# Upper-triangle self-products of 4096 rows: batch rows adjacent on a partition, 64 KB store packets, three large buffers, and single-row instructions shared by VectorE and ScalarE

## The chip, the cores and the metric

One core of one Trainium2 chip. The metric is the device time of one execution in microseconds; executions of a kernel agree here within 0.07%. All runs quoted are at full granted clock. Profiles are of one execution; its span, from first to last instruction, is about 1.8 us below the device time.

## The reference, cut to what matters

```python
def reference(inputs):                       # float32 [4096, 256]
    dot = jnp.einsum('bi,bj->bij', inputs, inputs)
    iu, ju = jnp.triu_indices(256)
    return dot[:, iu, ju]                    # float32 [4096, 32896]
```

Row i of the triangle of one batch row is `x[i] * x[i:256]`, a run of 256 - i products. The input has 4.19 MB, the output 538.97 MB: this is a kernel that writes.

## The kernel before

The batch rows are cut into 8 groups of 4 tiles of 128 rows. A partition holds four rows that are 128 rows apart in HBM, and a chunk is 2048 columns (the last 2176) of them. So one store of 4 MB consists of 512 separate runs of 8 KB. Four buffers rotate.

```python
x_in = x.rearrange("(g t p) d -> g p t d", t=GROUP, p=P)
x_out = out.rearrange("(g t p) c -> g p t c", t=GROUP, p=P)
# ... all eight x tiles are loaded at the start ...
for g in range(groups):
    xt = xs[g]
    for c, (lo, hi) in enumerate(zip(borders, borders[1:])):
        o = opool.tile([P, GROUP, widest], F32, tag="o", name=f"o_{g}_{c}")
        for i, j, col, length in runs(d, lo, hi):
            a = col - lo
            if length <= SHORT:              # 64: one VectorE instruction for four rows
                nc.vector.tensor_tensor(...)
                continue
            for t in range(GROUP):           # else one per row, every fourth on ScalarE
                # ... dst, src, factor ...
                if t == GROUP - 1:
                    nc.scalar.activation(dst, src, AF.Copy, scale=factor)
                else:
                    nc.vector.tensor_scalar(dst, src, factor, None, ALU.mult)
        nc.sync.dma_start(x_out[g][:, :, lo:hi], o[:, :, : hi - lo])
```

Of the kernel before, what the change touches and what calls it, by code (L numbers as in the profile page):

```python
# [1 line left out]

# [4 lines left out]

F32 = mybir.dt.float32
AF = mybir.ActivationFunctionType
ALU = mybir.AluOpType  # L10

P = 128
UNIT = 128      # columns: chunk borders are multiples of it, 512 bytes in HBM
CHUNKS = 16     # pieces that an output row is cut into
GROUP = 4       # batch tiles of 128 rows that are computed and stored together
SHORT = 64      # runs up to this length take one instruction for the whole group


def chunk_borders(width: int) -> list[int]:
    units = width // UNIT  # L20
    borders = [units * c // CHUNKS * UNIT for c in range(CHUNKS)]
    return borders + [width]


def runs(d: int, lo: int, hi: int):
    """The runs of output columns [lo, hi) with one first factor: (i, j, column, length), for
    x[i] * x[j : j + length]. Row i of the upper triangle has j from i on."""
    at = 0
    for i in range(d):
        a, b = max(at, lo), min(at + d - i, hi)  # L30
        if a < b:
            yield i, i + a - at, a, b - a
        at += d - i


@with_exitstack
def kernel(
    ctx: ExitStack, tc: tile.TileContext, x: bass.AP, out: bass.AP
):
    """out[n, :] = the upper triangle, row by row, of the outer product of x[n] with itself.  # L40

    Batch rows lie on the partitions. The input stays on chip; the output is made chunk by chunk
    and each chunk goes out in one store while the next ones are computed."""
    nc = tc.nc
    n, d = x.shape
    width = out.shape[1]
    assert n % (P * GROUP) == 0 and width == d * (d + 1) // 2 and width % UNIT == 0
    groups = n // (P * GROUP)
    borders = chunk_borders(width)
    widest = max(b - a for a, b in zip(borders, borders[1:]))  # L50

    xpool = ctx.enter_context(tc.tile_pool(name="x", bufs=1))
    opool = ctx.enter_context(tc.tile_pool(name="o", bufs=4))

    x_in = x.rearrange("(g t p) d -> g p t d", t=GROUP, p=P)
    x_out = out.rearrange("(g t p) c -> g p t c", t=GROUP, p=P)

    xs = []
    for g in range(groups):
        xt = xpool.tile([P, GROUP, d], F32, tag=f"x{g}", name=f"x{g}")  # L60
        nc.sync.dma_start(xt, x_in[g])
        xs.append(xt)

    for g in range(groups):
        xt = xs[g]
        for c, (lo, hi) in enumerate(zip(borders, borders[1:])):
            o = opool.tile([P, GROUP, widest], F32, tag="o", name=f"o_{g}_{c}")
            for i, j, col, length in runs(d, lo, hi):
                a = col - lo
                if length <= SHORT:  # L70
                    nc.vector.tensor_tensor(  # L71
                        o[:, :, a : a + length],
                        xt[:, :, j : j + length],
                        xt[:, :, i : i + 1].to_broadcast([P, GROUP, length]),
                        ALU.mult,
                    )
                    continue
                for t in range(GROUP):
                    dst = o[:, t, a : a + length]
                    src = xt[:, t, j : j + length]  # L80
                    factor = xt[:, t, i : i + 1]
                    # Of four such instructions one goes to the Scalar engine.
                    if t == GROUP - 1:
                        nc.scalar.activation(dst, src, AF.Copy, scale=factor)  # L84
                    else:
                        nc.vector.tensor_scalar(dst, src, factor, None, ALU.mult)  # L86
            nc.sync.dma_start(x_out[g][:, :, lo:hi], o[:, :, : hi - lo])  # L87


# [1 line left out]
_INS = ["r_inputs"]  # L91
_OUTS = [((4096, 32896), "float32")]


# [20 lines left out]
```

## Time and profile before

| | before |
|---|---|
| device time, median of 4 | 1312.78 us (1312.46 to 1312.98) |
| VectorE / ScalarE instructions | 5272 / 1553 |
| data packets on the store queue | 71808, most of 8 KB |
| output stores | 128, 4 buffers |

The lines that carry the argument stand in the prediction. Two more parts of the page, first the chain of work that ended last (shares of the span by engine), then the three large groups of instructions (line, engine, operation, shapes, count, busy us, mean ns, idle us before them):

```profile
DMA 54%; DVE 43%; issue 0%; DVEq 0%; SPq 0%
...
L86 DVE TENSOR_SCALAR o<-x 128x256 f32<-128x256 f32 (+44 forms) x4656 | 989.7, 291 | 111.4 <-DMA out_dram<-o 106.9
L84 ACT ACTIVATE o<-x 128x105 f32<-128x105 f32 (+59 forms) x1552 | 503.5, 411 | 764.4 <-DMA out_dram<-o 762.0
L71 DVE TENSOR_TENSOR o<-x 128x112 f32<-128x112 f32 (+51 forms) x616 | 137.1, 284 | 60.0 <-DMA out_dram<-o 60.0
```

The chain's 43% of VectorE looks like a second bound; the prediction says why it is not one.

### The profile page before, as it was taken

How to read it: one execution, taken by the hardware profiler on the slowest of the kernel's cores; microseconds unless marked ns; L12 is line 12 of the kernel's file. 1: busy time of each engine (PE TensorE's matmuls, PEld its weight loads, DVE VectorE, ACT ScalarE, POOL GpSimd, SP SyncE). 2: the span in 40 equal slices, each digit the busy share in tenths (PEclk: the TensorE clock that was granted, in tenths of full speed). 3: DMA queues.
4: the chain of work that ended last, by engine and by line, in shares of the span. 5: the costliest groups of instructions: out<-in, count | busy, mean ns of one | idle time of the engine just before them, and what ended most of it. 6: DMA issues, size and time to landing. Idle time of an engine off the chain costs nothing.

```text
span 1310.8 us, 7383 instructions
## 1 busy us (share of the span) xinstructions
DVE 1116.7 (85%) x5272; ACT 504.8 (39%) x1553; POOL 0.2 (0%) x4
## 2 busy tenths in 40 slices
DVE  8889977899778997789977899778996789967893
ACT  5345234442344423345333443334433443334430
POOL 0000000000000000000000000000000000000000
DMA  9999999999999999999999999999999999999996
GB/s 370 428 428 421 420 419 419 419 420 419 419 419 419 420 419 420 419 419 419 419 420 419 419 419 419 419 418 419 420 419 419 419 419 418 420 419 419 419 419 274
DMA packets 71865, 543.64 MB, mean 415 GB/s; under 512 B 2176, under 2 KB 6272, under 8 KB 6272
## 3 DMA queue, kind: packets, MB, share of 16 engines
q1 hardware_dynamic: 71808, 543.17, 100.0%
q14 instruction: 57, 0.47, 0.1%
HBM read 4.19 MB, written 538.97 MB: 414 GB/s over the span
## 4 chain that ended last, share of the span: by engine, by line
DMA 54%; DVE 43%; issue 0%; DVEq 0%; SPq 0%
DMA out_dram<-o 54%; DVE o L86 34%; DVE o L71 9%; DMA x<-in_r_inputs_dram 0%; DVEq L71 0%; DVEq L86 0%; SPq L87 0%; DVEq L111 0%
## 5 line engine op out<-in xcount | busy, mean ns | idle before, releaser
L86 DVE TENSOR_SCALAR o<-x 128x256 f32<-128x256 f32 (+44 forms) x4656 | 989.7, 291 | 111.4 <-DMA out_dram<-o 106.9
L84 ACT ACTIVATE o<-x 128x105 f32<-128x105 f32 (+59 forms) x1552 | 503.5, 411 | 764.4 <-DMA out_dram<-o 762.0
L71 DVE TENSOR_TENSOR o<-x 128x112 f32<-128x112 f32 (+51 forms) x616 | 137.1, 284 | 60.0 <-DMA out_dram<-o 60.0
L84 ACT ACT_TABLE_LOAD x1 | 1.3, 1283 | 0.7 <-PEq L102 0.7
L102 POOL MEMSET const-bfloat16-1.0<- 128x1 bf16 x1 | 0.1, 102 | 0.0
L102 POOL MEMSET const-uint8-127<- 128x1 uint8 x1 | 0.1, 101 | 0.0
L102 POOL MEMSET const-float32-0.0<- 128x1 f32 x1 | 0.1, 98 | 0.2 <-issue 0.2
L102 POOL MEMSET const-float32-1.0<- 128x1 f32 x1 | 0.1, 98 | 0.0
## 6 DMA issues: line engine op xcount, KB each, us to landing
out_dram<-o SPq DMA_DIRECT2D x120, 4096.0 KB, 31.5
out_dram<-o SPq DMA_DIRECT2D x8, 4352.0 KB, 22.6
x<-in_r_inputs_dram SPq DMA_DIRECT2D x8, 512.0 KB, 8.6
```

The costliest lines, as they stand in the source:

```text
L71: nc.vector.tensor_tensor(o[:, :, a : a + length], xt[:, :, j : j + length], xt[:, :, i : i + 1].to_broadcast([P, GROUP, length]), ALU.mult,)
L84: nc.scalar.activation(dst, src, AF.Copy, scale=factor)
L86: nc.vector.tensor_scalar(dst, src, factor, None, ALU.mult)
L102: nc = _bacc.Bacc("TRN2", target_bir_lowering=False, num_devices=1)
```

## The change

The intent is long contiguous packets. A partition takes 32 adjacent batch rows, whose output is one contiguous stretch of 4 MiB + 16 KiB. It is cut into 64 chunks of 64.8 or 65.0 KB per partition after a first tile that goes out in four growing pieces. Three buffers of 64 KB per partition hold 192 KB. Rows in a chunk no longer line up, so every product row is one instruction; a running cost estimate gives it to VectorE or ScalarE. The diff, cut to its core:

```diff
-    xpool = ctx.enter_context(tc.tile_pool(name="x", bufs=1))
-    opool = ctx.enter_context(tc.tile_pool(name="o", bufs=4))
-    x_in = x.rearrange("(g t p) d -> g p t d", t=GROUP, p=P)
-    x_out = out.rearrange("(g t p) c -> g p t c", t=GROUP, p=P)
+    xpool = ctx.enter_context(tc.tile_pool(name="x", bufs=3))
+    opool = ctx.enter_context(tc.tile_pool(name="o", bufs=3))
+    x_in = x.rearrange("(p r) d -> p r d", p=P)
+    x_out = out.rearrange("(p r) c -> p (r c)", p=P)
 ...
+SLOT = 16384
+FIRST = [1024, 3072, 7168, 15360]
+ROWS = 4
 ...
+    def multiply(self, dst, src, factor, length: int):
+        v = self.vector + 130 + 0.51 * length
+        s = self.scalar + 187 + 0.83 * length
+        if v <= s:
+            self.vector = v
+            self.nc.vector.tensor_scalar(dst, src, factor, None, ALU.mult)
+        else:
+            self.scalar = s
+            self.nc.scalar.activation(dst, src, AF.Copy, scale=factor)
 ...
+    borders = [0] + even_borders(FIRST[-1], total, -(-rest // SLOT))
+    for c, (lo, hi) in enumerate(zip(borders, borders[1:])):
+        if lo // width // ROWS > len(xs) - 3:
+            load()                           # the next four input rows of each partition
+        o = opool.tile([P, SLOT], F32, tag="o", name=f"o_{c}")
+        cuts = [0] + FIRST if c == 0 else [lo, hi]
+        for a, b in zip(cuts, cuts[1:]):
+            shares.even()
+            for row, i, j, at, length in runs(d, a, b):
+                # ... shares.multiply(...) ...
+            nc.sync.dma_start(x_out[:, a:b], o[:, a - lo : b - lo])
```

More of the change, by code (lines that the diff above doesn't have):

```diff
@@ L12, with even_borders, __init__, even @@
 P = 128
-UNIT = 128
-CHUNKS = 16
-GROUP = 4
-SHORT = 64
-def chunk_borders(width: int) -> list[int]:
-    units = width // UNIT
-    borders = [units * c // CHUNKS * UNIT for c in range(CHUNKS)]
-    return borders + [width]
-def runs(d: int, lo: int, hi: int):
-    at = 0
-    for i in range(d):
-        a, b = max(at, lo), min(at + d - i, hi)
-        if a < b:
-            yield i, i + a - at, a, b - a
-        at += d - i
+UNIT = 64
+def even_borders(lo: int, hi: int, pieces: int) -> list[int]:
+    units = (hi - lo) // UNIT
+    return [lo + units * c // pieces * UNIT for c in range(pieces)] + [hi]
+def runs(d: int, lo: int, hi: int):
+    width = d * (d + 1) // 2
+    for row in range(lo // width, (hi + width - 1) // width):
+        at = row * width
+        for i in range(d):
+            a, b = max(at, lo), min(at + d - i, hi)
+            if a < b:
+                yield row, i, i + a - at, a, b - a
+            at += d - i
+class Shares:
+    def __init__(self, nc):
+        self.nc = nc
+        self.vector = self.scalar = 0.0
+    def even(self):
+        self.vector = self.scalar = 0.0
+    def multiply(self, dst, src, factor, length: int):
[10 more added lines that the diff above has]
+ROWS = 4
 @with_exitstack
@@ L46 @@
     width = out.shape[1]
-    assert n % (P * GROUP) == 0 and width == d * (d + 1) // 2 and width % UNIT == 0
-    groups = n // (P * GROUP)
-    borders = chunk_borders(width)
-    widest = max(b - a for a, b in zip(borders, borders[1:]))
-    xpool = ctx.enter_context(tc.tile_pool(name="x", bufs=1))
-    opool = ctx.enter_context(tc.tile_pool(name="o", bufs=4))
-    x_in = x.rearrange("(g t p) d -> g p t d", t=GROUP, p=P)
-    x_out = out.rearrange("(g t p) c -> g p t c", t=GROUP, p=P)
-    xs = []
@@ L59 @@
-    for g in range(groups):
-        xt = xpool.tile([P, GROUP, d], F32, tag=f"x{g}", name=f"x{g}")
-        nc.sync.dma_start(xt, x_in[g])
-        xs.append(xt)
-    for g in range(groups):
-        xt = xs[g]
-        for c, (lo, hi) in enumerate(zip(borders, borders[1:])):
-            o = opool.tile([P, GROUP, widest], F32, tag="o", name=f"o_{g}_{c}")
-            for i, j, col, length in runs(d, lo, hi):
-                a = col - lo
-                if length <= SHORT:
-                    nc.vector.tensor_tensor(
-                        o[:, :, a : a + length],
-                        xt[:, :, j : j + length],
-                        xt[:, :, i : i + 1].to_broadcast([P, GROUP, length]),
-                        ALU.mult,
-                    )
-                    continue
-                for t in range(GROUP):
-                    dst = o[:, t, a : a + length]
-                    src = xt[:, t, j : j + length]
-                    factor = xt[:, t, i : i + 1]
-                    if t == GROUP - 1:
-                        nc.scalar.activation(dst, src, AF.Copy, scale=factor)
-                    else:
-                        nc.vector.tensor_scalar(dst, src, factor, None, ALU.mult)
-            nc.sync.dma_start(x_out[g][:, :, lo:hi], o[:, :, : hi - lo])
@@ new lines, with load @@
+    assert n % P == 0 and width == d * (d + 1) // 2
+    per = n // P
+    total = per * width
+    assert per % ROWS == 0 and total % UNIT == 0
+    xpool = ctx.enter_context(tc.tile_pool(name="x", bufs=3))
+    opool = ctx.enter_context(tc.tile_pool(name="o", bufs=3))
+    x_in = x.rearrange("(p r) d -> p r d", p=P)
+    x_out = out.rearrange("(p r) c -> p (r c)", p=P)
+    xs = []
+    def load(first_apart: bool = False):
+        g = len(xs)
+        if g * ROWS >= per:
+            return
+        xt = xpool.tile([P, ROWS, d], F32, tag="x", name=f"x_{g}")
+        cuts = [0, 1, ROWS] if first_apart else [0, ROWS]
+        for a, b in zip(cuts, cuts[1:]):
+            nc.sync.dma_start(xt[:, a:b, :], x_in[:, g * ROWS + a : g * ROWS + b, :])
+        xs.append(xt)
@@ new lines @@
+    load(first_apart=True)
+    load()
+    load()
+    rest = total - FIRST[-1]
+    borders = [0] + even_borders(FIRST[-1], total, -(-rest // SLOT))
+    shares = Shares(nc)
+    for c, (lo, hi) in enumerate(zip(borders, borders[1:])):
+        if lo // width // ROWS > len(xs) - 3:
+            load()
+        o = opool.tile([P, SLOT], F32, tag="o", name=f"o_{c}")
+        cuts = [0] + FIRST if c == 0 else [lo, hi]
+        for a, b in zip(cuts, cuts[1:]):
+            shares.even()
+            for row, i, j, at, length in runs(d, a, b):
+                xt, r = xs[row // ROWS], row % ROWS
+                shares.multiply(
+                    o[:, at - lo : at - lo + length],
+                    xt[:, r, j : j + length],
+                    xt[:, r, i : i + 1],
+                    length,
+                )
+            nc.sync.dma_start(x_out[:, a:b], o[:, a - lo : b - lo])
```

## The prediction

> **What bounds the kernel now.** I read the page first, then the waits, then a table of windows over chosen stretches, then the last stretch microsecond by microsecond. The page's busy shares, its DMA rows and its issue rows:
>
> ```profile
> span 1310.8 us, 7383 instructions
> DVE 1116.7 (85%) x5272; ACT 504.8 (39%) x1553; POOL 0.2 (0%) x4
> DMA  9999999999999999999999999999999999999996
> q1 hardware_dynamic: 71808, 543.17, 100.0%
> q14 instruction: 57, 0.47, 0.1%
> out_dram<-o SPq DMA_DIRECT2D x120, 4096.0 KB, 31.5
> ```
>
> The reader is to see that the 16 DMA engines are full in every slice but the last, while VectorE has 15% and ScalarE 61% to spare. A 4 MB store takes 4194304 / 419 GB/s = 10.0 us of the engines, and 31.5 us from issue to landing, so three stores are always in flight. The waits say the same from the other side:
>
> ```profile
> ACT o L84 <- DMA out_dram<-o: 762.0, 124, 10.3
> DVE o L86 <- DMA out_dram<-o: 106.9, 46, 3.9
> DVE o L71 <- DMA out_dram<-o: 60.0, 35, 3.4
> ```
>
> Both compute engines wait for stores to give buffers back, so the chain's "DVE 43%" is the chain hopping through compute that the transfers cover; it is not a share that a faster VectorE would save. The windows (columns: stretch, us, VectorE busy, ScalarE busy, GpSimd busy, TensorE clock, DMA share, GB/s):
>
> ```profile
> 30.00:100.00 70.00, 61.34 (x281) 29.20 (x89) 0.00 (x0) 1.00 1.01 427
> 110.00:1280.00 1170.00, 1011.90 (x4795) 452.79 (x1403) 0.00 (x0) 1.00 1.01 419
> 1289.00:1299.00 10.00, 0.00 (x0) 0.00 (x0) 0.00 (x0) 1.00 1.01 421
> 1300.00:1310.00 10.00, 0.00 (x0) 0.00 (x0) 0.00 (x0) 1.00 0.07 29
> ```
>
> Three things matter here. The rate is 427 to 428 GB/s at first and 419 from about 110 us on, with the DMA engines full in both. It stays at 421 after all compute has stopped (1289 to 1299), so VectorE and ScalarE don't cause the loss. And in the last 10 us the DMA share is 0.07, about 1/16: one DMA engine alone is still writing. The end of the kernel is that one engine's.
>
> From the trace's DMA records: the last engine, alone, starts a packet of 8704 bytes every 324.7 ns. [...] For 8192 bytes this is 305.9 ns, or 428 GB/s on 16 engines: the early rate exactly. At 419 GB/s it is 312.8 ns. So a steady packet loses 6.9 ns to something that is not there early and not there when an engine runs alone. I call it interference.
>
> [...] queue 14 moved 57 packets, nearly all of 8192 bytes, each about 309 ns, on the same DMA engines as the stores.
>
> The last point explains the lone engine. VectorE's 5272 instructions at 64 bytes (0.47 MB over 7383 instructions) are 41 packets, 41 x 0.309 = 12.7 us. If all go through one DMA engine, it falls behind by that. In the completion records of the stores, the last engine trails the median one by 1.8 us at 90 us and by 11.5 us at the end.
>
> A check of the whole on that engine: 2 us to the first data, input 10.8 us [...], 4112 output packets x 312.8 ns = 1286, instruction fetch 12.7: 1311.7 against a span of 1310.8. The sum holds within 1 us.
>
> **The change part by part.**
>
> 1. Packets. A partition holds 32 rows that follow each other in HBM, so a chunk of 16192 or 16256 columns is one run of 64.8 or 65.0 KB. Per DMA engine the output needs about 64 x 8 + 4 x 8 = 544 packets in place of 4112. Saved: 3568 x 4.7 ns = 16.8 us. This I hold for nearly certain if the packets are really that long.
>
> 2. Interference. 6.9 ns x 4112 = 28 us today. Does it go by packet or by byte? [...] Against that: early in the run it is absent at the same load[...]. I take half: 14 us saved, and mark it as the widest term.
>
> 3. Compute. Sorting the new kernel's product runs as its rule does gives 4959 instructions for VectorE and 3300 for ScalarE (the compiled orders agree to a few). Slopes: the trace's first 24 VectorE instructions (249 to 256 elements) took 6.34 us, 264 ns each, and the first 35 ScalarE ones 13.33 us, 381 each; the rule's 130 + 0.51 L and 187 + 0.83 L give 259 for L = 252, and about 395 for L = 250, so it is honest. The sums are 968 and 965 us: 15.0 us per chunk on average, 11 for the long half of a row and 19.0 for the short half, never more than 30.0 for two chunks in succession. A store of 8.29 MB takes 19.1 to 19.8 us. With 3 buffers compute has nearly two store times for each chunk, plus slack for the lagging engine (12 us). Nothing on the path; VectorE drops to about 75%, ScalarE rises to about 75%.
>
> 4. Start. First input is 128 KB, so compute starts near 3.0 us in place of 4.4. Pieces of 1024, 2048, 4096 and 8192 columns take 0.8, 1.4, 2.7 and 5.7 us to compute and 1.2, 2.4, 4.8 and 9.7 to store (at 0.43 MB per us), behind 1.7 MB of input (until about 6 us). The fourth piece is stored until about 24.5 us. The next chunk takes 15.6 us of compute after 13.6, so it is ready at 29.2 and moves about 1.2 us after issue (the first load of the old kernel took that long). All DMA engines idle for about 6 us. The old kernel has no such gap. Cost: +6 us.
>
> 5. [...] Instruction fetch on the lagging engine 4959 x 64 bytes = 39 packets, 0.7 us saved.
>
> Sum: 1310.8 - 16.8 - 14 + 6 - 0.9 - 0.7 = 1284.4 us of span; the timed runs were 1.9 us above the span, so 1286. I name 1285.
>
> **The rivals.**
> - Interference stays by byte. Then term 2 is 0 and the time about 1299, 1% faster. [...]
> - Interference goes as in the first 100 us. Then term 2 is 28 and the time about 1272, 3% faster. [...]
> - [...]
> - Compute becomes the bound at the short halves: 19.0 us against 19.4. Only if instructions run some 30% longer than in the trace would it show; the average of 15.0 leaves room.
> - Instruction fetch has to queue behind 64 KB packets (2.4 us each) on its DMA engine. At 200 ns per instruction an 8 KB packet lasts 25 us, so this should stay hidden.
>
> **Range and chances.** 1272 and 1299 are the two ends of the widest term; the start gap may be wrong by 4 us. So 1264 to 1303 should hold 8 times in 10. The 2% line is 1312.7 x 0.98 = 1286.4, almost at my middle. As long packets can hardly make the interference worse, and the start pieces look tuned, I put slightly more below it: faster 0.53, same 0.43, slower 0.04.
>
> **What would show it right or wrong.** Queue 1 with about 9,000 to 10,000 packets of near 65 KB (right for term 1). A steady rate in the windows: 425 means by byte, 429 to 430 my half, 433 to 434 interference gone. DMA tenths with a dent near 25 to 30 us (term 4). Waits of both compute engines for stores, with no waits of the store queue's transfers for compute after the start (term 3). One DMA engine alone for about 10 us at the end (fetch). [...]

The sum came to 1284.4 us of span, 1286 of time. All its terms still stand in it, but the line of one (0.9 us) and the working behind others are cut. What the numbers are worth by the trace records:

- 4.7 ns per packet. An engine that works alone starts a packet of 8704 bytes every 324.7 ns (kernel before, from 1302 us on) and one of 65024 bytes every 2395.3 ns (changed kernel, from 1279 us on). The difference is 0.036765 ns per byte; 8704 bytes are 320.0 ns, and 4.7 ns are left for the packet itself; 8192 bytes then take 305.9 ns. Below, clean means these two numbers.
- Input. 10.8 us in the check is an estimate from them for 256 packets of 1 KB on an engine. The 0.9 us of term 5, whose line is cut, is an estimate too: 192 packets fewer on an engine, at 4.7 ns.
- Interference. Of the 8 KB packets on the store queue before, 95% have the clean record of 309 ns from 30 to 100 us; from 110 to 1280 us 15% do, and 312, 314 and 316 ns are the usual times beside it (6.8 ns over 309 on the mean). What it goes by was not shown then: the half, 14 us, was my guess.

One rival is cut whole; the 0.04 for slower was my guess for it.

## The result, and the profile after

The changed kernel takes 1291.84 us (median of 4, 1291.77 to 1292.48) against 1312.78: ratio 0.9842, 95% interval 0.9829 to 0.9856. A ratio here is the mean time of one kernel's fast runs over that of the other's of the same rounds, so not quite the ratio of the medians. It is a real gain of 1.6%, within the 2% band. The prediction was 1285, with 1264 to 1303 as its range.

The rows of the page that answer to those shown of before:

```profile
span 1290.1 us, 8579 instructions
DVE 975.8 (76%) x4959; ACT 968.9 (75%) x3301; POOL 0.2 (0%) x4
DMA  7999999999999999999999999999999999999994
q1 hardware_dynamic: 11088, 543.17, 97.7%
q14 instruction: 66, 0.54, 0.1%
DMA 68%; DVE 28%; ACT 1%; issue 0%; DVEq 0%; SPq 0%; ACTq 0%
out_dram<-o SPq DMA_DIRECT2D x48, 8096.0 KB, 45.2
```

The packets on the store queue fell from 71808 to 11088, as intended, and VectorE and ScalarE share the work evenly at three quarters of the span. The waits:

```profile
ACT o L52 <- DMA out_dram<-o: 279.4, 59, 8.6
DVE o L49 <- DMA out_dram<-o: 271.5, 59, 8.6
```

Both engines still wait for stores only. The windows (stretch, us, VectorE busy, ScalarE busy, GpSimd busy, TensorE clock, DMA share, GB/s):

```profile
24.00:26.00 2.00, 2.00 (x13) 2.00 (x9) 0.00 (x0) 1.00 0.16 66
26.00:28.00 2.00, 2.00 (x13) 2.00 (x9) 0.00 (x0) 1.00 0.00 0
28.00:30.00 2.00, 2.00 (x14) 2.00 (x10) 0.00 (x0) 1.00 0.00 0
30.00:32.00 2.00, 2.00 (x16) 2.00 (x11) 0.00 (x0) 1.00 1.21 518
...
110.00:400.00 290.00, 224.11 (x1137) 222.05 (x754) 0.00 (x0) 1.00 1.00 431
400.00:800.00 400.00, 301.03 (x1530) 298.55 (x1018) 0.00 (x0) 1.00 1.00 433
800.00:1260.00 460.00, 349.89 (x1791) 347.11 (x1193) 0.00 (x0) 1.00 0.99 426
...
1272.00:1277.00 5.00, 0.00 (x0) 0.00 (x0) 0.00 (x0) 1.00 0.18 78
1280.00:1289.00 9.00, 0.00 (x0) 0.00 (x0) 0.00 (x0) 1.00 0.05 22
```

A packet's bytes are counted where it starts, and one now lasts 2.4 us, so windows of a few us swing (518 GB/s is no real rate); the long ones are sound. Three things are to be seen. All DMA engines idle before 30 us, as predicted: by the DMA records the first engine runs dry at 24.1 us, the median one at 25.0 and the last at 25.7, and they go on at 30.15. The steady rate is 431 to 433 GB/s, not the 419 of before, and it sinks to 426 in the last third. And from about 1270 us on only three DMA engines work, from 1280 us on only one. The stretch in which the median engine is done and some engine still works has grown from 10 to 18 us.

The trace's completion records (one time per DMA engine and store) tell the rest. The table gives by how much the last DMA engine trails the median one:

```
            early            middle            late              last store but one
before      1.8 us at 105    5.2 us at 600     9.9 us at 1037    11.5 us at 1300
after       1.0 us at 51     12.0 us at 603    19.8 us at 938    19.2 us at 1270
```

In the changed kernel the median engine does a store of 8096 KB in 19.1 us. The instructions come in packets of their own: queue 14 of the profile, of the kind "instruction", moved 0.54 MB for 8579 instructions, 64 bytes each, and 66 of its packets in the span are of 8192 bytes. One of these, 128 instructions, is called a page here. Of the 66, 65 start 3 to 4 ns before the record of a store's packet ends, which is how packets follow each other on the lone engine too (one every 2395 ns, records of 2399): pages and stores share the DMA engines. The last engine does a store in 19.07 us when no page of VectorE's instructions falls into it, and in 19.86 us when one does. So a page costs that engine 0.79 us. The DMA records show where: the page's own packet takes 0.309 us, and the next data packet on the same engine takes 0.445 to 0.465 us longer than a clean one (2389 ns for 64768 bytes). There are 39 such cases, as many as VectorE has pages (4959 x 64 bytes / 8 KB = 38.7). A second kind, 24 cases with 0.11 to 0.21 us, fits ScalarE's 26. The records don't name engines, so the two kinds are told apart by count and by size. But from the second full store on all 63 stores agree: the last engine takes over 19.5 us for 37 of them, and these are the ones into which a page of the first kind falls. What the third laggard carries, no run shows.

From about 940 us on the lag stays near 19 to 20 us, one store. A buffer goes back only when the last engine has written its part, and compute starts just then (at 1094.3 us after a last completion at 1094.2). With three buffers the others run dry before the next chunk is computed and issued. Then they wait, which is the 426 GB/s: by the records 16.0 of the 16 engines are at work on the mean from 110 to 800 us, and 15.8 from 940 to 1250. One store is no fixed limit of the lag: in pe_fetch2 below it was 29 us for a while.

Two theories follow. **F (fetch):** the end is set by the one DMA engine that also fetches VectorE's instructions, and every page lengthens the kernel. **R (rate):** the end is set by the mean rate of the 16 engines, which depends on packets, layout and gaps; instruction counts are nothing to it.

### The profile page after: what moved, and what is told of

It is laid out like the page before. It is cut to its first block, busy times and chain, and to the rows that moved or that the text cites. A ratio compares the mean times of both kernels' runs of the same rounds, so it can differ in the third digit from the quotient of the medians.

```text
span 1290.1 us, 8579 instructions
## 1 busy us (share of the span) xinstructions
DVE 975.8 (76%) x4959; ACT 968.9 (75%) x3301; POOL 0.2 (0%) x4
## 3 DMA queue, kind: packets, MB, share of 16 engines
q1 hardware_dynamic: 11088, 543.17, 97.7%
## 4 chain that ended last, share of the span: by engine, by line
DMA 68%; DVE 28%; ACT 1%; issue 0%; DVEq 0%; SPq 0%; ACTq 0%
DMA out_dram<-o 67%; DVE o L49 28%; ACT o L52 1%; DMA x<-in_r_inputs_dram 0%; DVEq L49 0%; SPq L118 0%; DVEq L142 0%; ACTq L52 0%
## 5 line engine op out<-in xcount | busy, mean ns | idle before, releaser
L49 DVE TENSOR_SCALAR o<-x 128x251 f32<-128x251 f32 (+61 forms) x4959 | 975.8, 289 | 274.5 <-DMA out_dram<-o 271.5
L52 ACT ACTIVATE o<-x 128x255 f32<-128x255 f32 (+56 forms) x3300 | 967.6, 387 | 280.4 <-DMA out_dram<-o 279.4
L52 ACT ACT_TABLE_LOAD x1 | 1.3, 1283 | 0.7 <-PEq L133 0.7
```

What stands on the lines that cost most here:

```text
L49: self.nc.vector.tensor_scalar(dst, src, factor, None, ALU.mult)
L52: self.nc.scalar.activation(dst, src, AF.Copy, scale=factor)
```

## The experiments

All gave correct results. Times are medians of 4 or 5 runs; the kernel before took 1312.66 to 1312.77 us in the same rounds.

| run | us | ratio to before | interval |
|---|---|---|---|
| more_vec | 1345.12 | 1.0246 | 1.0231 to 1.0262 |
| cut_runs | 1298.43 | 0.9891 | 0.9876 to 0.9905 |
| equal | 1291.52 | 0.9838 | 0.9824 to 0.9853 |
| no_gap | 1287.06 | 0.9804 | 0.9788 to 0.9821 |
| small_packets | 1315.64 | 1.0022 | 1.0007 to 1.0036 |
| before_half | 1309.22 | 0.9973 | 0.9958 to 0.9988 |
| split15 | 1316.95 | 1.0031 | 1.0014 to 1.0048 |
| pe_fetch2 | 1317.58 | 1.0037 | 1.0023 to 1.0051 |
| both | 1282.31 | 0.9768 | 0.9755 to 0.9782 |
| both46 | 1280.07 | 0.9752 | 0.9738 to 0.9765 |

By the 2% rule both and both46 are faster than the kernel before, more_vec is slower, no_gap is unclear (its interval holds 0.98), and the others are the same. The comparisons below are between runs of different rounds; in these, the kernel before moved by 0.1 us.

### more_vec: idle VectorE instructions (failed as an experiment)

```diff
             nc.sync.dma_start(x_out[:, a:b], o[:, a - lo : b - lo])
+            if c > 0:
+                for _ in range(20):
+                    nc.vector.memset(pad[:, 0:1], 0.0)
```

> The changed kernel with 20 one-column memsets on VectorE added per chunk, 1280 in all, 10 more pages of 8 KB of instructions; data and transfers unchanged. Theory F (the end is set by the one DMA engine that also fetches VectorE's instructions, 0.76 us per page in the changed kernel's trace): 10 x 0.76 = 7.6 us longer, 1299 us, and the lone engine at the end trails by more. Theory R (the mean rate of the 16 engines sets the end, VectorE's count is nothing to it): 1291 to 1292. VectorE stays off the path: 15.0 + 20 x 0.1 = 17 us per chunk against 19.1 per store.

It took 1345 us, far more than either theory. Nothing depends on the memsets, and all 1280 of them (59 ns each) ran in the first 496 us, ahead of their place; ScalarE waited for them for 60.9 us. The windows of this run:

```profile
100.00:500.00 400.00, 326.17 (x2453) 266.05 (x906) 0.00 (x0) 1.00 0.86 367
600.00:1200.00 600.00, 460.77 (x2339) 457.11 (x1557) 0.00 (x0) 1.00 1.00 433
```

Up to 500 us the DMA share is 0.86: there compute did not keep up. It says nothing about F. The next run asks the same with instructions that can't be moved.

### cut_runs: more VectorE instructions, same data

```diff
             self.vector = v
+            if self.cut < 20 and length >= 32:      # 20 per chunk, from the third chunk on
+                self.cut += 1
+                self.vector += 130
+                h = length // 2
+                self.nc.vector.tensor_scalar(dst[:, :h], src[:, :h], factor, None, ALU.mult)
+                dst, src = dst[:, h:], src[:, h:]
             self.nc.vector.tensor_scalar(dst, src, factor, None, ALU.mult)
```

> The changed kernel, where from the third chunk on the first 20 VectorE runs of a chunk are cut in two: some 940 more VectorE instructions (5900 in all, the rule hands some runs to ScalarE for it), real ones that can't be moved ahead as the memsets of the failed run were. Start, data and packets as in the changed kernel. Theory F (DMA engine that fetches for VectorE ends last, 0.76 us a page): 7.4 pages, 5.6 us longer, 1297.5. Theory R (mean rate of the engines): 1292.

VectorE had 5902 instructions, ScalarE 3618. The time was 1298.43 us: 6.6 us more than the changed kernel, where F said 5.6 and R nothing. Of the last engine's 64 full stores 46 took over 19.5 us, where the changed kernel has 38: 8 x 0.79 = 6.3 us, nearly all of it. The lag of the last engine reached one store at 800 us in place of 940. The lone tail in this run's windows:

```profile
1279.00:1296.00 17.00, 0.00 (x0) 0.00 (x0) 0.00 (x0) 1.00 0.06 27
```

A DMA share of 0.06 is one engine of 16; by the completion records the second to last engine was done at 1282.9 us, the last at 1295.7. R falls as the sole cause of the end: bytes, packets and layout are those of the changed kernel, and compute was done long before.

### equal: fewer VectorE instructions, more on ScalarE

```diff
-                shares.multiply(dst, src, factor, length)
+                if k in vector:      # the longer half of the piece's runs
+                    nc.vector.tensor_scalar(dst, src, factor, None, ALU.mult)
+                else:
+                    nc.scalar.activation(dst, src, AF.Copy, scale=factor)
```

> The changed kernel with equal instruction counts: in each piece the longer half of the runs goes to VectorE, the shorter to ScalarE, 4130 each. Theory F: VectorE's pages fall from 39 to 32, 7 x 0.76 = 5.3 us shorter, 1286.5 us; ScalarE's DMA engine gets 32 pages in place of 26 and stays behind it. Theory R: 1292, or longer if ScalarE (up to 20 us in a short half) now comes late.

1291.52 us, only 0.3 us less, which looks like R. But the lag grew more slowly, to 14.9 us at 919 us of the span where the changed kernel has 18.8 (at 918). What it won was lost at the start. The idle stretch of this run's windows:

```profile
24.00:26.00 2.00, 2.00 (x11) 2.00 (x9) 0.00 (x0) 1.00 1.22 524
26.00:28.00 2.00, 2.00 (x9) 2.00 (x9) 0.00 (x0) 1.00 0.00 0
28.00:30.00 2.00, 2.00 (x9) 2.00 (x9) 0.00 (x0) 1.00 0.00 0
30.00:32.00 2.00, 2.00 (x9) 2.00 (x10) 0.00 (x0) 1.00 0.00 0
32.00:34.00 2.00, 2.00 (x9) 2.00 (x11) 0.00 (x0) 1.00 0.00 0
34.00:36.00 2.00, 2.00 (x9) 2.00 (x11) 0.00 (x0) 1.00 1.21 518
```

The first full chunk was stored by 55.1 us in place of 50.8 us: 4.3 us lost. That left open whether the later 5 us are real; the run both settles it.

### no_gap: the idle start

```diff
-        cuts = [0] + FIRST if c == 0 else [lo, hi]
+        cuts = [0] + FIRST if c == 0 else [lo, lo + 8192, hi] if c == 1 else [lo, hi]
```

> The changed kernel, where the second chunk is stored as two pieces (8192 columns, then the rest). In the changed kernel all DMA engines are idle from 24.2 to 30.2 us. The first piece is computed by about 21.5 us, before the engines run dry. If the gap lies on the path of the engine that ends last: 6 us shorter, 1286. If something later gives it back (a buffer, VectorE): 1292.

1287.06 us, 4.8 less than the changed kernel. The same stretch of its windows:

```profile
24.00:26.00 2.00, 2.00 (x13) 2.00 (x9) 0.00 (x0) 1.00 0.69 295
26.00:28.00 2.00, 2.00 (x14) 2.00 (x9) 0.00 (x0) 1.00 1.18 508
28.00:30.00 2.00, 2.00 (x15) 2.00 (x10) 0.00 (x0) 1.00 1.10 475
```

The gap is gone, and it lay on the path of the engine that ends last. In the completion records the median engine is 5.3 us ahead after the second chunk and gives back 0.5 us in the third. The 6 us expected were read from windows, which count a packet where it starts; from the packets' ends the gap of the median engine was 5.2 us.

### small_packets: the new layout with 8 KB packets

```diff
-            nc.sync.dma_start(x_out[:, a:b], o[:, a - lo : b - lo])
+            for u in range(a, b, 2048):
+                w = min(u + 2048, b)
+                nc.sync.dma_start(x_out[:, u:w], o[:, u - lo : w - lo])
```

> The changed kernel's layout, buffers and compute, but each store issued as pieces of 2048 columns, 8 KB packets. Theory P (4.7 ns per packet and nothing else depends on packet length): about 3600 more packets on each engine, 17 us longer, 1309, and a store of the engine ahead still at the clean 19.09 us + 0.26 = 19.4. Theory I (the loss of 6.9 ns per packet of the kernel before belongs to short packets too): the median engine needs 19.9 us for a store, and the total is up to 1312. Theory L (the layout did it, not packet length): 1292.

1315.64 us, 23.8 more than the changed kernel, and the steady rate is again that of the kernel before:

```profile
110.00:1250.00 1140.00, 852.83 (x4334) 845.71 (x2883) 0.00 (x0) 1.00 1.01 419
```

So packet length, not the layout, gave the higher rate. From the DMA records, the mean time beyond a clean packet, per 8 KB:

```
before          6.8 to 6.9 ns   (16% of packets clean)
small_packets   4.1 to 5.6 ns   (about half clean)
after           1.4 to 2.1 ns
```

Theory I holds for the larger part: most of the interference comes with short packets, some of it with the old layout. (Its total, up to 1312, was 4 us too low.) The sum: 3600 packets x 4.7 ns = 16.9 us; 452 more completion packets of 9 ns on each engine (529 stores and loads in place of 77), up to 4.1 us; about 3 us are left. They are a net figure: what interference adds on the engine that ends last, and what its pages may cost less among short packets (next run), are not told apart here.

### before_half: fewer VectorE instructions in the kernel before

```diff
-                    if t == GROUP - 1:
+                    if t >= GROUP // 2:
```

> The kernel before with two of four long runs on ScalarE in place of one: VectorE 3720 instructions in place of 5272, 12 pages fewer, ScalarE 3104 in place of 1552, 12 more. Packets, layout and stores as before. Theory F: a page costs the lagging engine about 1.0 us there (its stores take 9.75 us without a page and 10.6 to 10.9 with one), 12 us less: 1301, with a shorter lone tail. Theory R: 1312 to 1313.

1309.22 us, 3.5 less, where F said 12. The direction is F's, the size is not. The lag at the last store but one fell from 11.5 to 8.2 us, by 3.3: nearly all of the gain is in the lag. The median engine's pace, 10.0 us per store, is that of before. But in this kernel the last engine wins part of a page's cost back. A stretch of its completion times (us per store of 4096 KB, from 498 to 578 us of the span):

```
last engine     9.79   9.90  10.00  10.02  10.92   9.71   9.77   9.85
median engine  10.04   9.99  10.00  10.02   9.98  10.03  10.00  10.02
```

A page (10.92) costs 0.9 us, and the next three stores are 0.2 to 0.3 us faster than the median engine's. The median engine stays at 10.0 us, with the interference; the one just behind it takes 9.71 to 9.85. So with short packets a page costs about 0.3 us net, as an estimate (3.5 us / 12 pages). In the changed kernel the last engine's stores without a page take 19.07 us, which is the clean time: there is no interference left to win back from, and a page costs its full 0.79 us. Why an engine that has just fallen behind escapes the interference, no run here shows.

### split15: which DMA engine is it? (backfired)

```diff
+            if c >= len(borders) - 3:
+                nc.sync.dma_start(x_out[0:120, a:b], o[0:120, a - lo : b - lo])
+                nc.sync.dma_start(x_out[120:128, a:b], o[120:128, a - lo : b - lo])
```

> The changed kernel, where each of the last two stores is issued as partitions 0 to 119 and 120 to 127. [...] If the lagging engine is the one left out: up to 38 us less on it, and the next laggard (11 us behind the rest) ends the kernel, 1283 to 1286. [...]

No trace or run here shows that an engine is left out at all: 1283 to 1286 is an estimate for that case, from two stores of 19.1 us. The run took 1316.95 us and located nothing: the last two stores ran at little more than half the rate.

```profile
1100.00:1200.00 100.00, 73.86 (x372) 73.06 (x246) 0.00 (x0) 1.00 0.99 427
1240.00:1280.00 40.00, 10.22 (x65) 9.97 (x44) 0.00 (x0) 1.00 0.94 242
```

The DMA share is 0.94, so the engines are not idle; each packet is slower (median 4.67 us for those that started in this window, in place of 2.40). No run here shows why. Which engine lags stays open.

### pe_fetch2: instructions of an engine that has nothing to do

```diff
+            if c > 0:
+                for _ in range(128):
+                    nc.tensor.matmul(acc, lhsT=wt, rhs=wt, start=True, stop=True)
```

> The run pe_fetch, which did not build, mended: the changed kernel with 16384 TensorE instructions that nothing waits for, 128 pages of 8 KB, 0.2% of the bytes. Theory F: one DMA engine that fetches them falls behind by 128 x 0.5 to 0.76 us and ends the kernel at 1328 to 1361, or at 1356 to 1389 if it is also VectorE's. Theory R (mean rate): 1294. If TensorE runs through its instructions early, the lag comes early and stays.

1317.58 us: 25.7 more than the changed kernel, for 0.2% more bytes. R's 1294 is out by 24 us; F's range, from 1328, was 10 too high. The windows, where two columns of TensorE (matmuls and weight loads) come first, and the page's queues:

```profile
30.00:400.00 370.00, 169.87 (x6501) 165.62 (x6498) 274.67 (x1400) 272.35 (x931) 0.00 (x0) 1.00 1.00 424
500.00:1250.00 750.00, 0.00 (x0) 0.00 (x0) 579.73 (x2946) 575.38 (x1962) 0.00 (x0) 1.00 0.99 426
...
q8 instruction: 64, 1.05, 0.3%
```

TensorE ran through its instructions in the first 454 us, over a queue of its own, in 64 transfers of 16 KB. While it did, the last engine needed about 21.1 us for a store in place of 19.1 and fell 29 us behind; afterwards it needs 19.3 to 19.6. From 52 to 456 us of the span it lost 39 us to 57 transfers, 0.7 us each. My range counted 128 transfers; there were 64. The last engine is another one than VectorE's here: with TensorE done it takes 19.3 to 19.6 us per store, not VectorE's pattern of 19.07 and 19.86.

The run shows one thing more. TensorE itself stood still for its fetches: 62 times, 237.9 us in total. The transfers came 7.2 us apart (median), the time of three 64 KB packets, and each block of 128 matmuls began about 2.4 us after one. VectorE's waits in the changed kernel show nothing of the kind: its pages came some 30 us apart, while TensorE was through a block in 3.4 us.

### both and both46: the two gains together

The start of no_gap, and from the third chunk on the longer half (in both46 the longest 46%) of a chunk's runs to VectorE:

```diff
+            order = sorted(range(len(piece)), key=lambda k: -piece[k][4])
+            vector = set(order[: int(len(order) * SHARE)])      # SHARE = 0.5 or 0.46
+                if c < 2:
+                    shares.multiply(dst, src, factor, length)
+                elif k in vector:
+                    nc.vector.tensor_scalar(dst, src, factor, None, ALU.mult)
+                else:
+                    nc.scalar.activation(dst, src, AF.Copy, scale=factor)
```

> The changed kernel with the second chunk stored in two pieces (worth 4.8 us alone) and equal instruction counts from the third chunk on (the run equal lost about 4.3 us at its start, because its idle gap there grew from 6 to 10 us, and gained about 5 later). Theory F: 1287.1 - 6 or 7 pages x 0.76 = 1282, the first to be 2% below the kernel before with room. If equal counts gained nothing: 1287.

1282.31 us: F's number. Against no_gap this is 4.8 us for 820 VectorE instructions fewer, 6.4 pages: 0.74 us per page. ScalarE got more work and more instructions, and the kernel got faster.

> As both, but 46% of the runs (the longest) to VectorE: 3790 instructions, about 29.6 pages in place of 32.3, ScalarE 4460, 35 pages at 0.5 us. Theory F: 2.7 x 0.76 = 2 us less than both, 1280, as long as ScalarE keeps up: its short halves take about 22 us against a store of 19.1, two chunks together 36 against 38. If it doesn't, longer than both, with waits of the store queue for ScalarE.

1280.07 us, F's number again and the fastest kernel, 2.5% below the kernel before. Its page:

```profile
DVE 849.0 (66%) x3798; ACT 1144.5 (90%) x4463; POOL 0.2 (0%) x4
```

A busy share of 90% on ScalarE would be called worse balance than 75 and 76%. But compute is not the bound; DMA engines are, and three of them now trail by nearly the same (14.3, 13.4 and 12.6 us at the last store, against 18.3, 9.0 and 5.8 in the changed kernel, where the others have waited for the first). For much of the run the last engine is not the one with VectorE's pages, so little more seems to be left this way. Its windows at the end:

```profile
1263.00:1277.00 14.00, 0.00 (x0) 0.00 (x0) 0.00 (x0) 1.00 0.15 65
```

0.15 is between two and three engines of 16.

## Why the prediction was right or wrong

The time, 1291.8, lies within the range, and "within 2%" had 0.43. It was 6.8 us above the named 1285. In part that is luck: of two errors of opposite sign, one was 9.0 us and the other 3.5. On the engine that ends last, the span divides so (clean is 0.036765 ns per byte plus 4.7 ns per packet, from the lone engines' records; "excess" is what that engine takes beyond clean for its stores):

| step | predicted | measured | how |
|---|---|---|---|
| packets | -16.8 | -16.7 | clean output 1257.7 us before, 1241.0 after |
| interference and pages | -14.7 | -5.7 | excess 35.6 before (1293.3 - 1257.7), 29.9 after (1258.8 from 30.3 us on - 1222.8 - 6.1 of input) |
| start and input | +5.1 | +1.6 | stores begin at 16.65 us before; after, 30.3 - 18.2 of stores done + 6.1 of input still to come = 18.2 |
| sum | -26.4 | -20.8 | last completion 1310.0 and 1289.1 |

Point by point:

1. **Packets: right.** 11088 packets, 4.7 ns each.
2. **Interference: right that it falls, wrong in size and reason.** I took it to halve. On the mean of the engines it fell by three quarters (from 6.9 ns per 8 KB to 1.4 to 2.1), and the rate rose to 431 to 433; on the last engine nothing is left of it. The reason that I gave was the layout. It does not hold for the larger part: small_packets has the new layout and 4.1 to 5.6 ns. The 14 us that I booked for it did not show, because pages took more (3).
3. **Instruction fetch: the step that failed.** I saw that one engine carries VectorE's 39 pages, and charged 0.309 us for each, the page's own packet, 12 us in all. It costs 0.76 by the packets (the data packet behind it loses 0.45 more) and 0.79 by the stores: 39 times that is 30 to 31 us, which is the whole excess of 29.9. I read the packet and not what came after it.
4. **The check that closed within 1 us was no proof.** In it, 28 us of interference and 12.7 of fetch filled a hole of 40. But the input took 4 us longer than I had (5), so the hole is 35.6. How it divides is not settled: at about 0.3 us net (before_half) the 41 pages are 12 of it, at the 0.9 that a store with a page takes longer they are nearly all. A sum that closes tells that the terms together are right, not each.
5. **Start gap: right, a little smaller** (5.2 us for the median engine where I had 6; removing it gave 4.8). The input was mis-sized: the old loads in 1 KB packets ended at 16.65 us, 14.8 us after the first data, where I had 10.8.
6. **Compute off the path: right.** Waits are for stores only. The rival "compute becomes the bound" is refuted by VectorE's 76% and ScalarE's 75%. With the new partition pitch of 4 MiB + 16 KiB the stores ran at 431 to 433 GB/s. My rival that fetches stay hidden behind 64 KB packets was right for VectorE, whose waits are for stores only, and missed that the data behind the fetch does not stay unharmed. For a faster reader of instructions it is wrong: TensorE stood still for 237.9 us in pe_fetch2.

## What to carry to other kernels

When a transfer-bound kernel ends with one DMA engine working alone, look at completion times engine by engine: here the mean rate was 431 to 433 GB/s for most of the run, and the last 18 us still belonged to engines that had fallen behind. Instructions are transfers too; with the long packets here every 128 VectorE instructions cost one DMA engine 0.79 us, so in such a kernel the number of instructions per engine is to be balanced, even at the price of a worse balance of busy time (both46: 1280.07 us against 1287.06 of no_gap). Long packets raised the rate here, from 419 GB/s to between 431 and 433, but made the start slower to fill (a gap of 5.2 us): let the first stores grow slowly enough that the engines don't run dry.
